# Layer 1 of a fused LSTM and quantum-circuit kernel: amplitude products on half arrays, nearest integers in SBUF, and two more buffers for low rows

## The chip, the cores and the metric

The kernel runs on one core of a Trainium2 chip. The metric is the device time of one execution in microseconds (us). The kernel before took 1453.79 us, the median of 3 runs (1453.73 to 1454.71).

## What is computed

The input x is 16 images of 128 channels and 64 x 64 pixels, f32. Two residual layers follow each other, each on a group-normalised input (32 groups of 4 channels, statistics over the image):

```python
x = x + _L0_conv_ref(_gn(x), ...)   # a diagonal LSTM: 127 dependent steps over skewed rows
x = x + _L1_conv_ref(_gn(x), ...)   # a 4-qubit circuit at every pixel
```

Layer 1 maps each pixel's 128 channels to 4 numbers, turns them into the angles of a product state of 4 qubits, applies a fixed circuit (16 complex amplitudes), takes the 4 expectations and maps them to 128 channels:

```python
xq = xf @ pre_w.T + pre_b
z = _simulate(xq, q_weights)
out = z @ post_w.T + post_b
```

The kernel writes the product state as a sum of sines of 8 signed sums of the angles. So a pixel needs 16 angles (a matmul), their sines, 32 amplitude parts (a matmul), their squares, and a last matmul to 128 channels, to which the residual is added.

## The kernel before, in words

Layer 0 takes about the first 1290 us: a load of all images with statistics, then a scan of 159 steps (`NSTEP`) whose order is written out by hand. It works in `ring`, an SBUF buffer of 40 of the 64 rows of all images. Rows 0 to 23 (`NLOW`) are finished first and stored to a DRAM buffer `low` (L605), so that later input rows can take their place. When the scan is done, rows 24 to 63 are in `ring` and rows 0 to 23 in `low`.

Beside the scan, VectorE collects the statistics of layer 1 in the tile `stats` (L122, bn_stats at L651). After the last step it reduces the last part (L628, L619, L621, L631), and a chain of small operations on VectorE, TensorE and ScalarE (L808 to L832) leaves `w_image` and `b_image`, the angle weights with the normalisation folded in.

Layer 1 goes image by image. A block of 8 rows is a tile of 128 x 512; an image has 8 of them, three low ones (`lowp`, 12 buffers) and five views of `ring`. For image b:

- `load(b)` (L848): GpSimd issues three DMAs from `low` to SBUF (L853), 256 KB each.
- `angles(b)` (L859): 8 matmuls into one PSUM tile `theta` (two buffers), each on a quarter of the array's columns, in the order of blocks 4, 6, 2, 0, then 5, 7, 3, 1. Blocks 0 to 2 are the low ones. The 128 partitions of `theta` are 8 blocks of 16 angles.
- `sines(b)` (L874): ScalarE adds `b_image` (L878); VectorE takes the nearest integer by adding and subtracting a large constant, into `theta`'s own PSUM tile (L879), and subtracts it (L880); ScalarE takes the sine (L883).
- `squares(b)` (L885): two matmuls of the full array (L889), `am0` and `am1`, each with all 128 partitions of sines as contraction; ScalarE squares both (L894). The weights `w_amp[:, h, :]` are zero outside the 64 partitions of half h, because each group of 16 partitions has its own 32 output columns (L462, `mask`).
- `outputs(b, h)` (L896): four matmuls into four PSUM tiles `po0` to `po3` (one buffer each), each on a quarter of the array's rows.
- `finish(b, h)` (L910): four VectorE operations (L917) add `po`, the bias and the residual in place, in the low tile or in `ring`. The sync engine SP stores each low tile by itself (L919) and the ring rows in one DMA per half (L922). A low tile's buffer comes free when its store has landed.

In the profile each f32 matmul is two MATMUL instructions (passes). The order of the stage is written out by hand (L927 to L955): the first four images are loaded ahead; then per image load(b+4), outputs(b,0), ScalarE's and VectorE's share of sines(b+2) around finish(b,0), squares(b+1), the sine of b+2, outputs(b,1), finish(b,1), angles(b+3). Each engine runs its instructions in that order. With 12 low buffers, the three loads of image b+4 take the buffers of the three low tiles of image b, in order.

Buffers of pools that are closed are given to pools that are opened later: `lowp`, `sinp` and `sqp` lie where the scan's pools lay, and their first writer waits for the last users there. `const` stays for the whole kernel.

Of the kernel before, what the change touches and what calls it, by code (L numbers as in the profile page):

```python
# [11 lines left out]
F32 = mybir.dt.float32  # L12
AF = mybir.ActivationFunctionType
ALU = mybir.AluOpType
PSUM = bass.MemoryType.PSUM

P = 128
NB = 16
# [8 lines left out]
CHUNK = 2 * BLOCK  # L27
# [8 lines left out]
ROUND = 12582912.0  # L36
# [43 lines left out]
def kernel(  # L80
# [16 lines left out]
    nc = tc.nc  # L97
# [3 lines left out]
    const = ctx.enter_context(tc.tile_pool(name="const", bufs=1))  # L101
# [17 lines left out]
    mean2 = const.tile([P, NB], F32, name="mean2")  # L119
    rstd2 = const.tile([P, NB], F32, name="rstd2")  # L120
    NG2 = NH // 4
    stats = const.tile([P, NB, NG2, 6], F32, name="stats")  # L122
    w_theta = const.tile([P, 128], F32, name="w_theta")
    w_image = const.tile([P, NB, 48], F32, name="w_image")
    b_image = const.tile([P, NB], F32, name="b_image")
# [1 line left out]
    w_amp = const.tile([P, 2, 128], F32, name="w_amp")  # L127
# [24 lines left out]
    with ExitStack() as scan:  # L152
        wpool = scan.enter_context(tc.tile_pool(name="wpool", bufs=1))
# [2 lines left out]
        w1T = wpool.tile([P, 512], F32, name="w1T")  # L156
        wsT = wpool.tile([P, 512], F32, name="wsT")
        bias = wpool.tile([P, 4], F32, name="bias")

        hinv = wpool.tile([P, NH], F32, name="hinv")  # L160
        cinv = wpool.tile([P, NH], F32, name="cinv")
# [36 lines left out]
        with ExitStack() as prep:  # L198
# [188 lines left out]
            for g in ORDER:  # L387
                first[g] = ps_gate.tile([P, 2, NC], F32, name=f"ps0_{g}", tag="gate")
                for w, rhs in ((w1T, hst[0][:, :, 0 : LEAST // 2]), (w0T, above(hst[0], 0, LEAST // 2))):
                    nc.tensor.matmul(  # L390
                        first[g][:, :, 0 : LEAST // 2],
                        lhsT=w[:, g * 128 : (g + 1) * 128],
                        rhs=rhs,
                        start=w is w1T,
                        stop=True,
# [398 lines left out]
        with tc.manual_schedule():  # L794
# [7 lines left out]
            k, n = 2 * FIRST, 2 * NG2  # L802
# [33 lines left out]

    lowp = ctx.enter_context(tc.tile_pool(name="lowp", bufs=12))
    sinp = ctx.enter_context(tc.tile_pool(name="sinp", bufs=3))  # L840
    sqp = ctx.enter_context(tc.tile_pool(name="sqp", bufs=2))
    ps_t = ctx.enter_context(tc.tile_pool(name="ps_t", bufs=2, space=PSUM))
    ps_a = ctx.enter_context(tc.tile_pool(name="ps_a", bufs=1, space=PSUM))
# [2 lines left out]
    x1s, ths, turns, sqs = {}, {}, {}, {}  # L846
# [27 lines left out]
    def sines(b):  # L874

        th = ths[b]
        y = sinp.tile([P, CHUNK], F32, name=f"y{b}", tag="y")
        nc.scalar.activation(y, th, AF.Identity, bias=b_image[:, b : b + 1])  # L878
        nc.vector.tensor_scalar(th, y, ROUND, ROUND, ALU.add, ALU.subtract)  # L879
        nc.vector.tensor_sub(y, y, th)  # L880
        turns[b] = y
        yield
        nc.scalar.activation(y, y, AF.Sin, scale=TWO_PI)  # L883

    def squares(b):  # L885
        ams = []
        for h in range(2):
            am = ps_a.tile([P, CHUNK], F32, name=f"am{b}_{h}", tag=f"am{h}")
            nc.tensor.matmul(am, lhsT=w_amp[:, h, :], rhs=turns[b], start=True, stop=True)  # L889
            ams.append(am)  # L890

        sqs[b] = [sqp.tile([P, CHUNK], F32, name=f"sq{b}", tag="sq"), turns[b]]
        for am, s in zip(ams, sqs[b]):
            nc.scalar.activation(s, am, AF.Square)  # L894
# [32 lines left out]
    with tc.manual_schedule():  # L927
        for b in range(4):
            load(b)
        angles(0)  # L930
        for _ in sines(0):
            pass
        angles(1)
        later = sines(1)
        next(later)
        squares(0)
        next(later, None)
        for b in range(NB):
            if b + 4 < NB:
                load(b + 4)  # L940
            po = outputs(b, 0)
            later = sines(b + 2) if 0 < b < NB - 2 else iter(())
            finish(b, 0, po)
            next(later, None)
            if b + 1 < NB:
                squares(b + 1)
            next(later, None)
            po = outputs(b, 1)
            finish(b, 1, po)
            if b == 0:  # L950
                angles(2)
                for _ in sines(2):
                    pass
            if b + 3 < NB:
                angles(b + 3)  # L955
# [37 lines left out]
```

## Time and profile before

| what | value |
|---|---|
| median of 3 runs | 1453.79 us |
| the profiled execution, its own time | 1455.38 us |
| its span in the profile | 1453.4 us |
| mean granted TensorE clock | 0.985 of full speed |
| TensorE matmul busy | 1371.0 us (94%) |
| VectorE busy | 976.8 us (67%) |
| ScalarE busy | 766.1 us (53%) |
| GpSimd busy | 897.6 us (62%) |
| HBM read, written | 59.61 MB, 46.14 MB |
| layer 1's first angle matmul starts at | 1304.1 us |
| first store of layer 1 | 1314.9 us |

How to read it: busy shares are of the whole span, of which the scan is nine tenths, so they say little about layer 1. For that stage one reads the timeline, the waits and windows from 1290 us on. In a timeline row stand start, length, engine, line, operation, output <- input, shape and count, and in square brackets the idle time before it and who ended it. The lines cited, such as L889, are those of the code above. PE is TensorE, PEld its weight loads, DVE VectorE, ACT ScalarE, POOL GpSimd, SP the engine that issues the stores.

### The profile page before, as it was taken

How to read it: one execution, taken by the hardware profiler on the slowest of the kernel's cores; microseconds unless marked ns; L12 is line 12 of the kernel's file. 1: busy time of each engine (PE TensorE's matmuls, PEld its weight loads, DVE VectorE, ACT ScalarE, POOL GpSimd, SP SyncE). 2: the span in 40 equal slices, each digit the busy share in tenths (PEclk: the TensorE clock that was granted, in tenths of full speed). 3: DMA queues.
4: the chain of work that ended last, by engine and by line, in shares of the span. 5: the costliest groups of instructions: out<-in, count | busy, mean ns of one | idle time of the engine just before them, and what ended most of it. 6: DMA issues, size and time to landing. Idle time of an engine off the chain costs nothing. (4 is left out here: it accounts for less than half of the span.)

```text
span 1453.4 us, 19718 instructions
## 1 busy us (share of the span) xinstructions
PE 1371.0 (94%) x5942; PEld 966.9 (67%) x5942; DVE 976.8 (67%) x2450; ACT 766.1 (53%) x1855; POOL 897.6 (62%) x1717
## 2 busy tenths in 40 slices
PE   6778999999999999999999999999999999858987
PEld 5648887766777667676677767776677787852222
DVE  6884566566665666877767775555555688768776
ACT  5545666555555555555555555555555565533221
POOL 4215787766777667788788766676666676531110
PEclk9999999999999999999999999999999999989997
DMA  9970000000000000144433000000000000027997
GB/s 327 362 263 1 1 1 1 1 1 1 1 0 1 1 0 1 59 136 136 134 117 116 1 0 1 2 0 1 1 1 0 1 1 1 1 88 259 332 326 269
DMA packets 86008, 107.00 MB, mean 74 GB/s; under 512 B 3936, under 2 KB 70528, under 8 KB 85904
## 3 DMA queue, kind: packets, MB, share of 16 engines
q1 hardware_dynamic: 80624, 92.29, 18.8%
q0 software_dynamic: 4048, 12.67, 2.7%
q8 instruction: 47, 0.77, 0.2%
q10 hardware_dynamic: 1232, 0.80, 0.2%
q14 instruction: 57, 0.47, 0.1%
HBM read 59.61 MB, written 46.14 MB: 73 GB/s over the span
## 5 line engine op out<-in xcount | busy, mean ns | idle before, releaser
L565 PE MATMUL ps<-xn,wxT 128*128 128x512 f32 (+18 forms) x1280 | 481.3, 519 | 1.5 <-POOL xn L556 0.9
L709 DVE TENSOR_TENSOR ps<-ps,both 128x256 f32<-128x256 f32 (+9 forms) x544 | 219.5, 408 | 318.6 <-PE ps L694 312.3
L713 ACT ACTIVATE ps<-ps,bias 128x512 f32<-128x512 f32 (+23 forms) x480 | 268.4, 581 | 254.1 <-DVE ps L709 217.5
L565 PEld LDWEIGHTS ps<-xn,wxT 128*128 128x128 f32 x1280 | 232.4, 192 | 174.9 <-issue 155.4
L739 ACT COPY both<-ps 128x256 f32<-128x256 f32 (+9 forms) x544 | 191.5, 355 | 179.9 <-PE ps L694 160.1
L694 PE MATMUL ps<-diff,w1T 128*128 128x256 f32 (+14 forms) x1088 | 284.3, 364 | 0.0
L694 PE MATMUL ps<-diff,w0T 128*128 128x256 f32 (+14 forms) x1088 | 284.1, 363 | 0.0
L599 POOL TENSOR_TENSOR ring<-ring,hst 128x256 f32<-128x256 f32 (+8 forms) x488 | 247.8, 539 | 24.4 <-DVE hst L776 24.4
L694 PEld LDWEIGHTS ps<-hst,wsT 128*128 128x128 f32 x1088 | 195.9, 190 | 86.7 <-DVE hst L776 38.1
L694 PE MATMUL ps<-hst,wsT 128*128 128x256 f32 (+14 forms) x1088 | 241.6, 365 | 6.6 <-DVE hst L776 5.0
L694 PEld LDWEIGHTS ps<-diff,w1T 128*128 128x128 f32 x1088 | 200.8, 191 | 21.0
L694 PEld LDWEIGHTS ps<-diff,w0T 128*128 128x128 f32 x1088 | 200.6, 191 | 21.0
L556 POOL TENSOR_TENSOR xn<-xn,rstd 128x512 f32<-128x512 f32 (+10 forms) x160 | 170.7, 1067 | 14.8 <-DVE rstd L149 2.3
L551 POOL TENSOR_TENSOR xn<-ring 128x256 f32<-128x256 f32 (+8 forms) x213 | 147.0, 700 | 0.0
L776 DVE TENSOR_TENSOR hst<-g,ps 128x256 f32<-128x256 f32 (+13 forms) x320 | 107.8, 368 | 46.6 <-ACT g L767 44.1
L546 POOL TENSOR_TENSOR xn<-ring,mean 128x16 f32<-128x16 f32 (+8 forms) x247 | 130.6, 538 | 11.4 <-DVE mean L139 10.4
L767 ACT ACTIVATE g<-cst 128x256 f32<-128x256 f32 (+20 forms) x320 | 102.9, 368 | 64.5 <-DVE cst L766 63.9
L590 POOL TENSOR_TENSOR diff<-hst 128x240 f32<-128x240 f32 (+9 forms) x136 | 102.9, 756 | 41.5 <-DVE hst L776 37.7
L766 DVE TENSOR_TENSOR cst<-cst,ps 128x256 f32<-128x256 f32 (+20 forms) x320 | 104.6, 368 | 5.5
L788 POOL COPY edge<-hst 128x16 f32<-128x16 f32 x64 | 25.1, 392 | 134.3 <-DVE hst L776 134.3
L763 DVE TENSOR_TENSOR ps<-ps,g 128x512 f32<-128x512 f32 (+20 forms) x160 | 95.1, 594 | 18.1 <-ACT g L713 17.1
L713 ACT ACTIVATE g<-ps,bias 128x512 f32<-128x512 f32 (+20 forms) x160 | 97.3, 608 | 11.5 <-PE ps L694 3.5
(309 smaller groups left out, 1218.3 us busy)
## 6 DMA issues: line engine op xcount, KB each, us to landing
out_dram<-ring SPq DMA_DIRECT2D x16, 1024.0 KB, 5.7
ring<-in_x_dram SPq DMA_DIRECT2D x15, 1024.0 KB, 10.1
rest<-in_x_dram SPq DMA_DIRECT2D x48, 256.0 KB, 7.8
low<-ring SPq DMA_DIRECT2D x6, 2048.0 KB, 7.6
ring<-in_x_dram SPq DMA_DIRECT2D x6, 2048.0 KB, 8.2
low<-low POOLq DMA_DIRECT2D x48, 256.0 KB, 5.2
out_dram<-low SPq DMA_DIRECT2D x48, 256.0 KB, 4.9
ring<-in_x_dram SPq DMA_DIRECT2D x20, 256.0 KB, 10.1
```

The lines of the kernel that those rows point to most:

```text
L546: nc.gpsimd.tensor_sub(by_pairs(xn, 0, j, n), x0, over(mean1, n))
L551: nc.gpsimd.tensor_sub(by_pairs(xn, 1, j, n), lower, of)
L556: nc.gpsimd.tensor_mul(v, v, r)
L565: nc.tensor.matmul(ps[g][:, :, a:b], lhsT=wxT[:, g * 128 : (g + 1) * 128], rhs=xns[t % 2][:, :, a:b], start=t > 0, stop=True, skip_group_c ...
L590: nc.gpsimd.tensor_sub(diff[:, 0, a1:b], now[:, 1, a1 - NB : b - NB], now[:, 0, a1:b])
L599: nc.gpsimd.tensor_add(x1, x1, by_pairs(new, q, j, n))
L694: nc.tensor.matmul(out, lhsT=w[:, g * 128 : (g + 1) * 128], rhs=rhs, start=False, stop=True, skip_group_check=True,)
L709: nc.vector.tensor_add(v, v, both[g][:, a:b])
L713: nc.scalar.activation(to[:, :, a:w], ps[g][:, :, a:w], FUNC[g], bias=bias[:, g : g + 1])
L739: nc.scalar.copy(both[g][:, a:b], ps[g][:, 0, a:b])
L766: nc.vector.tensor_add(c[:, q], c[:, q], ig[:, q])
L776: nc.vector.tensor_mul(new[:, q, a:v], th[:, q, a:v], act[GO][:, q, a:v])
```

## The change

Four edits, in layer 1's buffers and two of its steps:

- The tile `stats` moves from the pool `const` to `wpool`, which is closed with the scan.
- `lowp` has 14 buffers in place of 12. The three loads of image b+4 so take the buffers of low tiles 1 and 2 of image b-1 and of tile 0 of image b.
- The nearest integers go to a new SBUF tile `near` (a pool of one buffer) in place of `theta`'s PSUM tile.
- Each of the two amplitude matmuls contracts only the 64 partitions on which its weights are not zero, on rows 0 to 63 or rows 64 to 127 of the array.

The order of the stage and the number of instructions stay as they were.

```diff
-    stats = const.tile([P, NB, NG2, 6], F32, name="stats")
...
         bias = wpool.tile([P, 4], F32, name="bias")
+        stats = wpool.tile([P, NB, NG2, 6], F32, name="stats")
...
-    lowp = ctx.enter_context(tc.tile_pool(name="lowp", bufs=12))
+    lowp = ctx.enter_context(tc.tile_pool(name="lowp", bufs=14))
     sinp = ctx.enter_context(tc.tile_pool(name="sinp", bufs=3))
+    nearp = ctx.enter_context(tc.tile_pool(name="nearp", bufs=1))
...
-        nc.vector.tensor_scalar(th, y, ROUND, ROUND, ALU.add, ALU.subtract)
-        nc.vector.tensor_sub(y, y, th)
+        near = nearp.tile([P, CHUNK], F32, name=f"near{b}", tag="near")
+        nc.vector.tensor_scalar(near, y, ROUND, ROUND, ALU.add, ALU.subtract)
+        nc.vector.tensor_sub(y, y, near)
...
-            nc.tensor.matmul(am, lhsT=w_amp[:, h, :], rhs=turns[b], start=True, stop=True)
+            k = 64 * h
+            nc.tensor.matmul(
+                am,
+                lhsT=w_amp[k : k + 64, h, :],
+                rhs=turns[b][k : k + 64, :],
+                start=True,
+                stop=True,
+                tile_position=(k, 0),
+            )
```

## The prediction

> **What bounds the kernel now.** I read the slices of the page first: TensorE fills the scan (1290 us) and the change leaves that alone. It touches layer 1, the last 150 us, and the few microseconds before. Then I read the list of waits from 1304 us on (who <- for whom: us in total, times, longest):
>
> ```profile
> POOL low L853 <- DMA out_dram<-low: 42.4, 4, 19.1
> DVE low L917 <- PE po L900: 24.4, 14, 5.0
> PE theta L864 <- DMA low<-low: 10.6, 8, 2.6
> ```
>
> VectorE is late because TensorE is, and TensorE because the low rows of a coming image have not landed; GpSimd, which issues those loads, waits for a store. The timeline of image 4 shows the ring (start, length, engine, operation; the last row is image 6):
>
> ```profile
> 1347.03 2.07 DVE L917 SCALAR_TENSOR_TENSOR low<-po,b_out,low 128x512 f32<-128x512 f32 x3 [3.87 <-PE po L900]
> 1353.48 1.78 POOL L853 DMA_DIRECT2D low<-low  x3 [7.24 <-DVE ring L917]
> 1361.08 0.62 PE L864 MATMUL theta<-low,w_image 128*32 128x512 f32 x2 [0.90 <-DMA low<-low]
> 1362.92 1.14 PE L900 MATMUL po<-sq,w_out 32*128 32x512 f32 x8
> 1364.08 2.07 DVE L917 SCALAR_TENSOR_TENSOR low<-po,b_out,low 128x512 f32<-128x512 f32 x3 [2.10 <-PE po L900]
> ```
>
> finish(4,0) starts at 1347.03; its first store lands and frees a low buffer at 1353.48 (6.45 later; GpSimd's label names VectorE, but the wait also holds the store's semaphore, and finish had long written the tile); three issues take 1.78; the third tile lands 5.8 after that, at 1361.08; angles(8) and outputs(6,0), behind it in TensorE's order, let finish(6,0) start 3.0 later. That is 17.05 us for two images, 8.5 each. VectorE alone would need 6.95 (finish 2 to finish 3: 1329.51 to 1336.46). From finish(3,0) at 1336.46 to finish(13,0) at 1425.74, ten images take 89.3 us. DMA is not far behind (window; TensorE, weight loads, VectorE, ScalarE, GpSimd busy; clock, DMA share, GB/s):
>
> ```profile
> 1350.00:1356.00 6.00, 5.62 (x29) 1.44 (x28) 4.38 (x8) 1.32 (x2) 1.61 (x3) 1.00 0.72 235
> 1356.00:1362.00 6.00, 5.10 (x25) 1.52 (x25) 5.95 (x10) 1.82 (x3) 0.00 (x0) 1.00 1.06 393
> ```
>
> It reaches 393 GB/s with loads and stores mixed and starves between. An image moves 2.10 MB out and 0.79 MB in: at 393 that is 7.3 us.
>
> The start and the tail, from the timeline:
>
> ```profile
> 1291.47 5.49 POOL L853 DMA_DIRECT2D low<-low  x10 [0.36 <-POOL ring L599]
> 1299.21 0.42 DVE L631 TENSOR_REDUCE more<-stats 128x16 f32<-128x192 f32 x1
> 1304.37 1.07 PE L864 MATMUL theta<-low,w_image 128*32 128x512 f32 x2
> 1310.35 0.63 ACT L883 ACTIVATE y<-y 128x512 f32<-128x512 f32 x1 [1.48 <-DVE y L880]
> 1311.03 1.98 PE L889 MATMUL am<-y,w_amp 128*128 128x512 f32 x4 [1.27 <-ACT y L883]
> 1434.47 3.56 PE L889 MATMUL am<-y,w_amp 128*128 128x512 f32 x4
> 1439.12 2.73 DVE L917 SCALAR_TENSOR_TENSOR ring<-po,b_out,ring 128x512 f32<-128x512 f32 x4 [3.78 <-PE po L900]
> ```
>
> The first loads go out at 1291.47, 13 us before angles(0) needs them. At the end VectorE waits 3.78 us for a chain that holds am of image 15, 3.56 us long because TensorE's clock reads 0.50 there.
>
> [...] Two 64-row tiles are not in the trace, but four 32-row ones are: the eight po passes take 1.14 us, four full-array am passes 1.98. [...] The trace has 0.69 for both, with a PSUM operand; [...] after a stall of some 2 us that ends at 1389, the clock reads 0.50 from 1390 to 1392.
>
> **The change, part by part.**
> *stats moves to the pool that dies with the scan.* The build of the new kernel shows that the first load (L853) now waits for VectorE's second L631 as well: the low buffers lie where stats lay. L631 ends at 1299.63 instead of a release at 1291.47, so all twelve first loads move by 8.3 us. low_2 of image 0 is the third issue, two issues of 0.55 later; in the trace before, the third issue started at 1292.57 and had landed by 1297.32, 4.75 us. New landing: 1299.63+0.1+1.1+4.75 = 1305.6, where TensorE takes it at 1304.37. Behind that wait stand the rest of angles(0), angles(1) and everything after. Cost 1.2 to 1.5[...]: take +1.3. [...] Images 1 to 3 load well ahead and need no time.
> *near in SBUF.* L879 0.69 to 0.43, -0.26 an image; L880 stays 0.69. [...] It counts where VectorE leads: the first image, finish 1 to 2, 2 to 3. [...] near has one buffer, but writer and reader are both on VectorE, in order: no wait. theta comes free earlier; nobody waits for that.
> So finish(3,0) stands at +1.3-3x0.26 = +0.5.
> *Fourteen low buffers.* Loads of image b+4 no longer wait for stores (b,0), (b,1), (b,2), but for (b-1,1), (b-1,2), (b,0). Only tile 2 is left in the ring, released by the same store that released tile 0. Two issues leave it: -1.2. The bytes of two tiles leave the queue ahead of it: another 0 to -1.5 (0.52 MB at 350 GB/s), and more pressure on DMA gives some back. I take -1.5 per two images, 0.75 each. Of the ten intervals two (finish 9 to 11, 6.85 and 6.94) are VectorE's and gain 0.26: 8x0.75+2x0.26 = -6.5. New mean (89.3-6.5)/10 = 8.3 us an image, 348 GB/s: below 393, so it fits. Bounds: -1 (DMA is already the limit) to -12 (7.7 us an image).
> *am on half the rows each.* In mid-stage its 1.98 us are hidden: outputs(b,1) behind it waits for VectorE to free po anyway (at 1349.75 for image 4, while am ended at 1348.93). If that cover were gone it would be worth 0.9. In the tail: 3.56 to about 2.0, -1.5, and near of image 15 -0.2: -1.7. The bounds: -0.9 if the clock is full there, 0 if the tiles don't overlap.
>
> **Sum.** +0.5-6.5-1.7 = -7.7. The profiled execution took 1455.38 (span 1453.4 and 2.0 around it): 1447.7. It stood 1.6 above the median 1453.79, so for the median: 1446.1, call it 1446.
>
> **Rivals.**
> 1. DMA is already the limit, and earlier loads only displace stores. For it: shares of 0.93 to 1.05 through most windows. Against: 235 GB/s at 1350 to 1356, 393 just after. Then -1 in place of -6.5: 1453.8+0.5-1-1.7 = 1451.6, call it 1452.
> 2. The clock, and slower. Halving am takes a second of array work from each image, some 6.1 to 5.2 us of 8.3; half-clock spells then come inside the stage. For it: the clock falls in the tail as soon as angles are gone, and at 1389 after one stall. Against: in most images it held 1.00 through stalls of up to 2.6 us, and stalls shrink. A cold image needs theta 3.7, am 2.1, po 2.1 twice: 10 us, 1.7 over the 8.3. It eats the gain from about five cold images; all ten cold are +17 on the forecast: 1463. With eight cold: 1446+13.6 = 1459.6, call it 1459.
> 3. The halves don't run beside each other, so that the edit of am does nothing: the tail keeps 1.5, 1447.5. For it: no 64-row tile in the trace. Against: po's four tiles do overlap.
>
> **How the numbers follow.** Forecast 0.63 (own range 1441 to 1450.5); rival 1 0.16; rival 2 0.11; rival 3 0.10. 0.2% is 2.9 us, about what a measurement of this kernel can tell from no change: faster means under 1450.9. The forecast, rival 3 and a small part of rival 1 give 0.75 faster; the rest of rival 1 0.14 same; rival 2 0.11 slower. The range takes in the forecast, its unknown costs and most of rival 1: 1440 to 1453.
>
> **What would show it.** First load after 1299.6; angles(0) held on low to about 1305.6; L879 0.43; am's four passes about 1.1 us; the gap from finish(b,0) to finish(b+2,0) 16 to 16.6 in place of 17 to 18; finish(13,0) near 1419.7. It is wrong if the images stay at 8.9 us with DMA shares over 1.0 (rival 1), if the clock reads under 0.9 in windows between 1330 and 1420 (rival 2), or if the start costs more than 3 us.

## The result, and the profile after

The changed kernel takes 1448.08 us (median of 5 runs, 1447.33 to 1449.15); the kernel before took 1454.71 beside it (5 runs, 1453.73 to 1455.90; the three runs named further up are among them). The ratio is 0.9952, with an interval of 0.9939 to 0.9965: some 6.6 us faster, where 1446 had been predicted against 1453.79, which is 7.8. The profiled execution took 1447.33 us, its span is 1445.3; the one profiled before took 1455.38. So the two profiled executions lie 8.05 us apart, 1.4 more than the medians, and the parts read off them below add up to more than the change is worth in the median. (The scan has 160 steps, not the 159 told above; nothing rests on it.)

The list of waits of the changed kernel from 1304 us on, the three rows that answer to those shown of before:

```profile
POOL low L854 <- DMA out_dram<-low: 30.7, 9, 7.4
DVE low L928 <- PE po L911: 21.1, 14, 5.1
PE theta L865 <- DMA low<-low: 8.2, 4, 2.5
```

In total all three waits are shorter, and all three are still there: the ring from store to load to angles is eased, not gone. The start and the tail in the timeline of the changed kernel:

```profile
1298.28 0.42 DVE L631 TENSOR_REDUCE more<-stats 128x16 f32<-128x192 f32 x1
1299.42 6.03 POOL L854 DMA_DIRECT2D low<-low  x11 [9.24 <-DVE moments L808]
1304.77 1.07 PE L865 MATMUL theta<-low,w_image 128*32 128x512 f32 x2
1310.26 0.63 ACT L885 ACTIVATE y<-y 128x512 f32<-128x512 f32 x1 [1.22 <-DVE y L882]
1310.94 1.13 PE L893 MATMUL am<-y,w_amp 64*128 64x512 f32 x4 [1.06 <-ACT y L885]
1427.00 2.08 PE L893 MATMUL am<-y,w_amp 64*128 64x512 f32 x4
1429.01 1.94 PE L911 MATMUL po<-y,w_out 32*128 32x512 f32 x8
1430.97 2.73 DVE L928 SCALAR_TENSOR_TENSOR ring<-po,b_out,ring 128x512 f32<-128x512 f32 x4 [3.11 <-PE po L911]
```

The first load goes out 8.9 us later, counted from the end of the scan (9.84 in place of 0.96), after the reductions of the statistics. am's four passes take 1.13 us where the full array took 1.98, and 2.08 in the tail, at half clock, where it took 3.56. The scan, which the change leaves alone, happened to end 0.93 us earlier in this execution than in the one of before; so I count layer 1 from the last operation of the scan on VectorE (start of `hst`, 1290.51 before, 1289.58 after):

| us from the end of the scan | before | after | difference | predicted |
|---|---|---|---|---|
| angles(0) take low rows | 13.86 | 15.19 | +1.33 | +1.3 |
| finish(3,0) starts | 45.95 | 46.59 | +0.64 | +0.5 |
| finish(3,0) to finish(13,0) | 89.28 | 82.35 | -6.93 | -6.5 |
| finish(13,0) to the end of VectorE's work | 21.65 | 20.79 | -0.86 | -1.7 |
| end of the span | 162.89 | 155.72 | -7.17 | -7.7 |

The last stores take 6.0 us after VectorE's last operation in both. The third row runs from the start of finish(3,0), shown further down, to that of finish(13,0), here before and after:

```profile
1425.74 2.07 DVE L917 SCALAR_TENSOR_TENSOR low<-po,b_out,low 128x512 f32<-128x512 f32 x3 [1.76 <-PE po L900]
```

```profile
1418.52 2.07 DVE L928 SCALAR_TENSOR_TENSOR low<-po,b_out,low 128x512 f32<-128x512 f32 x3 [0.42 <-PE po L911]
```

Each figure of this table is from one execution a kernel. Other profiles with fourteen buffers, below, give 81.89 to 84.81 us in the third row.

### The profile page after: what moved, and what is told of

The parts are those of the page before. It is cut to its first block, busy times and chain, and to the rows that moved or that the text cites. A ratio compares the mean times of both kernels' runs of the same rounds, so it can differ in the third digit from the quotient of the medians.

```text
span 1445.3 us, 19732 instructions
## 1 busy us (share of the span) xinstructions
PE 1364.7 (94%) x5942; PEld 964.2 (67%) x5942; DVE 972.1 (67%) x2450; ACT 764.1 (53%) x1855; POOL 897.7 (62%) x1717
```

## The experiments

Each ratio is to the kernel before on the same chip, with its interval. "Images 3 to 13" and "tail" are the third and fourth row of the table, from the profile. The medians of the kernel before differ by chip and hour from 1454.7 to 1458.0 us, so only ratios are compared between chips.

**e1_twelve**: the changed kernel with 12 low buffers.

```diff
-    lowp = ctx.enter_context(tc.tile_pool(name="lowp", bufs=14))
+    lowp = ctx.enter_context(tc.tile_pool(name="lowp", bufs=12))
```

> The changed kernel with 12 low buffers again; near, am on half rows and the moved statistics stay. Ring theory (the fourteen buffers bring the gain): the images from finish(3,0) to finish(13,0) go back to about 8.9 us each, the start still costs about 0.7, the tail gains 0.9: 0 to 1 above the kernel before, 1454 to 1456 us. Rival (the cheaper VectorE and TensorE work brings the gain, the buffers little): it stays near the changed kernel, 1448 to 1450.

Measured: 1.0005 (0.9993 to 1.0016), as the ring theory expected. Images 3 to 13 take 91.58, even more than before. The other three edits without the buffers gain nothing.

**e2_only14**: the kernel before with 14 low buffers, and with `stats` in the pool of the scan, as in the changed kernel.

```diff
-    stats = const.tile([P, NB, NG2, 6], F32, name="stats")
...
+        stats = wpool.tile([P, NB, NG2, 6], F32, name="stats")
...
-    lowp = ctx.enter_context(tc.tile_pool(name="lowp", bufs=12))
+    lowp = ctx.enter_context(tc.tile_pool(name="lowp", bufs=14))
```

> The kernel before with the statistics moved and 14 low buffers alone: am on the full array, nearest integers in PSUM. Ring theory: nearly the whole gain, about -6.9 between images 3 and 13, +1.1 at the start, tail as before: 1448.5 to 1450. Rival (am and near bring it): within 1 us of the kernel before or slower by the start.

Measured: 0.9967 (0.9957 to 0.9976), images 3 to 13 84.81, tail 22.61. The buffers alone carry 0.33% of the changed kernel's 0.48%. Images 3 to 13 gained 4.5 in this profile, where 6.9 had been expected. The intervals from finish 1 to 2 and from 2 to 3 are 6.85 and 6.94, as before.

**e3_only_am**: the kernel before with am on half the rows each, nothing else.

```diff
-            nc.tensor.matmul(am, lhsT=w_amp[:, h, :], rhs=turns[b], start=True, stop=True)
+            k = 64 * h
+            nc.tensor.matmul(
+                am, lhsT=w_amp[k : k + 64, h, :], rhs=turns[b][k : k + 64, :],
+                start=True, stop=True, tile_position=(k, 0),
+            )
```

> The kernel before with am on half rows alone. If am is hidden in mid-stage and counts only in the tail: am of image 15 falls from 3.56 to about 2.1 us, but the array then stays at half clock through the following po, so that the tail gains 0.5 to 1: about 1454. Clock rival (less array work lets the clock fall in mid-stage): windows under 0.9 between 1330 and 1420 us and a time of 1456 or more. Rival that am sits on the ring: -0.9 for each of ten images, 1445.

Measured: 1.001 (1.000 to 1.002); images 3 to 13 89.52, as before. The time and the windows are those that the text above gives for the clock rival, not the 1454 of the first theory. Where TensorE waits longest, and the windows around it (window; TensorE, weight loads, VectorE, ScalarE, GpSimd busy; clock, DMA share, GB/s):

```profile
1344.88 1.07 PE L864 MATMUL theta<-low,w_image 128*32 128x512 f32 x2 [3.01 <-DMA low<-low]
```

```profile
1338.00:1344.00 6.00, 3.88 (x14) 1.17 (x12) 5.64 (x9) 1.71 (x3) 0.60 (x2) 0.94 1.02 341
1344.00:1350.00 6.00, 5.12 (x20) 1.08 (x20) 0.00 (x0) 0.69 (x1) 1.61 (x3) 0.50 1.06 368
...
1368.00:1374.00 6.00, 4.68 (x20) 0.98 (x24) 2.77 (x5) 0.87 (x2) 1.60 (x3) 0.72 1.07 393
```

TensorE waits for low rows across the first two windows, the clock falls to 0.50, and in the second VectorE does nothing for all 6 us. In the profile of before no window between 1320 and 1428 is under 0.82; here and in e1_twelve windows of 0.50 and of 0.72 to 0.73 lie in the stage. One such stall makes an interval of 13.41 us from one finish to the next (13.65 in e1_twelve; before, the longest is 11.69).

The mean granted clock of all executions, profiled or not, says the same. On this chip it is 0.984 over 50 executions of the kernel before, 0.980 over 22 of e3 and 0.981 over 14 of e1, but 0.985 over 21 of e2, which keeps the full am; the standard error of each is under 0.001. So with twelve buffers halving am lowers the clock. These means are of the whole span; for where it falls there are only the profiles: between finish(3,0) and finish(13,0) the clock is at half for 3.4 us before, for 10.2 here and for 17.0 in e1.

**e4_low15**: 15 low buffers, the nearest integers back in PSUM; `near`'s place in SBUF goes to the fifteenth.

```diff
-    lowp = ctx.enter_context(tc.tile_pool(name="lowp", bufs=14))
+    lowp = ctx.enter_context(tc.tile_pool(name="lowp", bufs=15))
...
-    nearp = ctx.enter_context(tc.tile_pool(name="nearp", bufs=1))
...
-        near = nearp.tile([P, CHUNK], F32, name=f"near{b}", tag="near")
-        nc.vector.tensor_scalar(near, y, ROUND, ROUND, ALU.add, ALU.subtract)
-        nc.vector.tensor_sub(y, y, near)
+        nc.vector.tensor_scalar(th, y, ROUND, ROUND, ALU.add, ALU.subtract)
+        nc.vector.tensor_sub(y, y, th)
```

> The changed kernel with 15 low buffers, for whose space the nearest integers go back to PSUM. The three loads of image b+4 then wait only for stores of image b-1, a whole image earlier. If the ring of store, load and angles still limits the changed kernel: the stalls ahead of low rows go, an image falls from 8.2 to 7.4 to 7.7 us, and the time to 1441 to 1444. If DMA bandwidth is now the limit (its share reads 1.02 to 1.07 in most windows): the mean image stays 8.1 to 8.3 us and the time 1447 to 1449.

Measured: 0.9907 (0.9890 to 0.9925), images 3 to 13 74.54. Its waits and its windows:

```profile
DVE low L926 <- PE po L909: 9.6, 14, 1.7
...
PE theta L864 <- DMA low<-low: 0.8, 2, 0.5
```

```profile
1350.00:1356.00 6.00, 6.00 (x36) 1.90 (x32) 5.80 (x10) 2.07 (x4) 1.61 (x3) 1.00 1.04 385
1356.00:1362.00 6.00, 6.00 (x28) 2.04 (x24) 5.80 (x10) 2.18 (x4) 1.07 (x2) 1.00 1.05 390
1362.00:1368.00 6.00, 6.00 (x31) 1.92 (x30) 4.84 (x9) 1.99 (x4) 0.54 (x1) 1.00 1.06 386
```

The wait of TensorE's matmuls for low rows fell from 8.2 us to 0.8, that of its weight loads, which come first, from 12.8 to 5.2. The DMA share stays over 1.0 in every window from 1338 to 1416, and 7.45 us an image with 2.88 MB is 387 GB/s: the limit that the prediction read off one window of before (393 GB/s, 7.3 us). So I take DMA to set the pace here, and not at fourteen buffers. That is argued: TensorE is busy for all of these windows too, and what speaks against it as the limit is e11 below, where 0.85 us more of its work in each image lengthens ten images by 1.4 us. A sixteenth buffer was not tried.

**e5_start**: the changed kernel with `stats` in a pool of its own that the low buffers don't overlie (opened first within the scan, with the sine pool opened ahead of `lowp`).

```diff
+        statp = scan.enter_context(tc.tile_pool(name="statp", bufs=1))
+        stats = statp.tile([P, NB, NG2, 6], F32, name="stats")
...
-        stats = wpool.tile([P, NB, NG2, 6], F32, name="stats")
...
-    lowp = ctx.enter_context(tc.tile_pool(name="lowp", bufs=14))
     sinp = ctx.enter_context(tc.tile_pool(name="sinp", bufs=3))
+    lowp = ctx.enter_context(tc.tile_pool(name="lowp", bufs=14))
```

> The changed kernel, but the statistics lie in a pool of their own, under the buffers of the sines, so that the first loads no longer wait for VectorE's last reduction. If that wait is what the start lost: first loads within 1 us of the scan's end, angles(0) takes low rows 0.3 us after the ring rows, finish(0,0) about 1.1 us earlier against the scan's end (23.3 in place of 24.3), and the whole 0.5 to 1.5 us faster than the changed kernel, 0.9945 of the kernel before. If the ring or DMA swallows the start: finish(13,0) and the time stay as in the changed kernel.

Measured: 0.9948 (0.9932 to 0.9964); the changed kernel beside it (e8) 0.9951. In its timeline the first load is back:

```profile
1291.32 5.50 POOL L855 DMA_DIRECT2D low<-low  x10 [0.36 <-POOL ring L600]
...
1304.21 1.07 PE L866 MATMUL theta<-low,w_image 128*32 128x512 f32 x2
```

From the end of the scan (1290.36 here), angles(0) take low rows at 13.85 and finish(3,0) starts at 45.29: 1.34 and 1.30 less than after the change. So the wait costs 1.3 us at the place, as told. The medians differ by 1.0, within the intervals.

**e6_tail**: the changed kernel with two more matmuls on the full array in the tail, whose result nobody reads, to keep the clock up for am of image 15.

```diff
+    def busy(n):
+        ps = ps_t.tile([P, CHUNK], F32, name="busy", tag="theta")
+        v = w_image.rearrange("p b a -> p (b a)")[:, 0:CHUNK]
+        for _ in range(n):
+            nc.tensor.matmul(ps, lhsT=w_out, rhs=v, start=True, stop=True)
...
+            elif b == NB - 3:
+                busy(2)
```

> The changed kernel with two full-array matmuls more, whose result nobody reads, after outputs(13,1), where the angles of the images before stood. If half clock is what keeps the tail long: the clock stays at 1.00 to the last am, am of image 15 takes 1.1 in place of 2.08 us, the po passes behind it 1.1 in place of 1.94, and from finish(13,0) to the last VectorE operation it is about 19.4 in place of 20.8 us. Rival (the tail is VectorE's, the clock only looks bad, and two more matmuls are in the way): 20.8 or more.

Measured: 0.9948 (0.9934 to 0.9962), 0.7 us under e8 on the same chip, which the intervals don't tell apart. The timeline of its tail:

```profile
1423.77 1.98 PE L942 MATMUL busy<-w_image,w_out 128*128 128x512 f32 x4
...
1427.47 1.13 PE L893 MATMUL am<-y,w_amp 64*128 64x512 f32 x4
...
1428.53 2.22 PE L911 MATMUL po<-y,w_out 32*128 32x512 f32 x8
```

am is at its 1.13 us. The po passes behind it take 2.22, not the 1.1 expected, but VectorE no longer waits for them: its operations follow each other without a gap there. VectorE ends 18.02 after finish(13,0), 2.8 sooner than after the change, but the last stores then need 7.24 us in place of 6.0: 1.2 of it went to the stores.

**e7_best**: 15 buffers without `near`, the statistics as in e5, the tail as in e6.

> 15 low buffers with the nearest integers in PSUM, the statistics' pool of the start experiment and the two extra matmuls in the tail, together. If the three add up: about 1.1 and 1.4 below the kernel with 15 buffers, 0.989 of the kernel before. If DMA, near its limit in the kernel with 15 buffers, takes the start's gain back: 0.990 to 0.991.

Measured: 0.9876 (0.9859 to 0.9892), 1437.44 us: it beats both kernels. Images 3 to 13 take 74.04.

**e8_changed_again**: the changed kernel, to share a chip with e5 to e7.

> The changed kernel as it is, beside the three above on the same chip: 0.995 of the kernel before, images 3 to 13 in 82 to 83 us, tail 20.8 us.

Measured: 0.9951 (0.9937 to 0.9965), as the first time.

**e9_no_near** and **e10_full_am**: the changed kernel without `near` (the last two hunks of e4), and the changed kernel with am on the full array (e3's edit undone).

> The changed kernel with the nearest integers back in theta's PSUM tile; 14 buffers and am on half rows stay. As predicted, near is worth 0.26 us where VectorE leads: finish(0,0) 0.3 to 0.5 later, the short intervals 6.94 in place of 6.84 us, 1 to 2 us slower than the changed kernel. What the runs so far suggest instead: the short intervals are a ring of TensorE and VectorE through the single po buffers, so that they stay at 6.85 without near, and only the first image loses; at most 0.7 us slower.

> The changed kernel with am on the full array again; 14 buffers and near stay. If am counts in the tail alone: am of image 15 takes about 3.5 us at half clock, the tail is 21.5 to 22.5 in place of 20.8 us, images 3 to 13 take 82 to 83.5 us, short intervals 6.9; 1 to 2 us slower than the changed kernel. If its time is on the ring too: images 3 to 13 take 85 us or more and it is 3 us slower or more.

Measured: 0.9947 (0.9931 to 0.9962) and 0.9940 (0.9920 to 0.9959). Neither edit is missed: taking either out costs nothing that shows, where 1 to 2 us had been expected for am and, by the prediction, for `near`. Images 3 to 13 are 84.57 and 82.92 in their profiles, against 82.35 and 83.01 in the two profiles of the changed kernel. In e10's tail am was expected at half clock, 3.5 us long; it is no longer than the halves were in the changed kernel:

```profile
1427.43 1.98 PE L892 MATMUL am<-y,w_amp 128*128 128x512 f32 x4
...
1429.35 1.14 PE L903 MATMUL po<-y,w_out 32*128 32x512 f32 x8
...
1430.51 2.73 DVE L920 SCALAR_TENSOR_TENSOR ring<-po,b_out,ring 128x512 f32<-128x512 f32 x4 [1.55 <-PE po L903]
```

The clock is 1.00 in its windows up to 1434, so am takes 1.98 and po 1.14, where the changed kernel had 2.08 and 1.94 at half clock. Its tail is 18.88 us, 1.9 shorter. That is one profile; e2's tail, also with the full am, was at half clock (am 3.78 us).

**e11_best_full_am** and **e12_best_no_tail**: e7 with am on the full array, and e7 without the two unread matmuls.

> The version with fifteen low buffers, nearest integers back in PSUM, statistics in a pool of their own and two unread matmuls in the tail, but with both amplitude products on the full array again (four passes 1.98 us in place of 1.13). Theory: in mid-stage am is hidden whatever the buffers, and DMA sets the pace with fifteen buffers (390 GB/s, 7.4 us an image), so images 3 to 13 take 74 to 75 us as with the halves; in the tail the clock is held, so am costs 0.9 more there at most. Time within 1 us of the version with halves, ratio to the kernel before 0.987 to 0.989. Rival: with the ring gone, TensorE's 0.9 us an image shows: 80 us or more for images 3 to 13, ratio 0.992 or above.

> The same version with the halved amplitude products, but without the two unread matmuls in the tail. Theory: the last VectorE operation comes 2 to 3 us later, because TensorE falls to half clock there, but the last stores then land in 6.0 us after it in place of 7.0 to 7.2[...]: 1 to 1.5 us slower than with them, ratio 0.988 to 0.989. Rival: the stores take the whole gain, no difference (0.9876).

Measured: 0.9878 (0.9864 to 0.9891) and 0.9894 (0.9879 to 0.9909). With am on the full array images 3 to 13 take 75.47, with the halves 74.04 and (e12) 76.87: with fifteen buffers too, am is hidden. Without the unread matmuls it is 3.3 us slower than e11 on the same chip and 2.6 slower than e7 by the ratios. The profile of e12, whose execution was the slowest of its five (1443.12), puts 2.8 in VectorE's tail and the last stores together (21.40 and 6.7, against 18.28 and 7.0 in e7). So the 1 to 1.5 expected was too low, though the intervals of e7 and e12 overlap a little.

## Why the prediction was right, point by point

**"Only tile 2 is left in the ring", 0.75 an image: right in cause, near in size.** 12 buffers in the changed kernel give back the whole gain (e1), 14 in the kernel before bring 0.33% (e2), 15 bring 0.44% more than the changed kernel (e4). Ten images gained 6.93 between the two profiles, predicted 6.5; against the same profile of before the others at fourteen buffers gain 4.5 to 7.4, so a match to 0.4 us is in part luck. The mean from finish to finish is 8.24 us, 16.5 for two images, as foretold (16 to 16.6). The ring in the changed kernel, image 4 to image 6:

```profile
1345.45 2.07 DVE L928 SCALAR_TENSOR_TENSOR low<-po,b_out,low 128x512 f32<-128x512 f32 x3 [2.86 <-PE po L911]
1354.05 1.64 POOL L854 DMA_DIRECT2D low<-low  x3 [7.43 <-DMA out_dram<-low]
1359.64 1.07 PE L865 MATMUL theta<-low,w_image 128*32 128x512 f32 x2 [2.26 <-DMA low<-low]
1363.99 2.07 DVE L928 SCALAR_TENSOR_TENSOR low<-po,b_out,low 128x512 f32<-128x512 f32 x3 [5.08 <-PE po L911]
```

The load that angles(8) wait for is now the first of the three that start at 1354.05 (tile 2 of image 8; the other two are tiles 0 and 1 of image 9), so the two issues are out of the ring, as told. It lands 5.6 later, at 1359.64. But the store before it took 8.6 us to land in place of 6.45: this is the worst pair, 18.54 us. Where it goes well nothing waits and VectorE's 6.84 stands: in the changed kernel one interval of 9.3 to 11.5 is followed by one or two of 6.84 to 7.04. The gain was foretold as an even 0.75; it came as fewer stalls.

**stats, +1.3: right.** +1.33 at angles(0); e5 takes 1.3 back at the place. That +0.64 at finish(3,0) lies near the predicted +0.5 is luck: the prediction took off 0.26 three times for `near`, and the profiles show 0.60, 0 and 0.10, of which the 0.60 is not `near`'s alone (next point). `b_image` starts at 13.43 from the end of the scan in place of 13.30, and one operation shows it, L815 with 0.31 us where it had 0.17. It has 0.31 in e1 and e4 too, but 0.17 in e2 and e10, and in e6 and e8, where the first loads go out 0.87 ahead of it as in the changed kernel: what lengthened it is not shown.

**near: the price right, the place wrong.** The groups of the changed kernel (busy us, mean ns | idle before):

```profile
L882 DVE TENSOR_TENSOR y<-y,near 128x512 f32<-128x512 f32 x16 | 11.1, 692 | 0.5
...
L881 DVE TENSOR_SCALAR near<-y 128x512 f32<-128x512 f32 x16 | 6.7, 419 | 8.4 <-ACT y L879 8.4
```

0.419 us, where 0.43 had been foretold; in the kernel before L879 and L880 both took 0.686 in the mean, and nothing in its trace showed the shorter time. But the step "It counts where VectorE leads: ... finish 1 to 2, 2 to 3" failed. Here is finish(3,0), two such intervals on, first in the changed kernel and then in the kernel before (the figure in brackets is the wait for po):

```profile
1336.17 2.07 DVE L928 SCALAR_TENSOR_TENSOR low<-po,b_out,low 128x512 f32<-128x512 f32 x3 [0.42 <-PE po L911]
```

```profile
1336.46 2.07 DVE L917 SCALAR_TENSOR_TENSOR low<-po,b_out,low 128x512 f32<-128x512 f32 x3 [0.20 <-PE po L900]
```

The wait for po grew from 0.20 to 0.42. The interval from finish 1 to 2 stayed at 6.84, and that from 2 to 3 fell from 6.95 to 6.85 only. The likely reason is that VectorE didn't lead there alone: po has one buffer each, so TensorE's next outputs wait for VectorE's finish and VectorE for them (from 1304 us on in the changed kernel, the weight loads for po wait 14.5 us for VectorE's low operations and 9.9 for its ring ones, VectorE 21.1 and 3.4 for po). With the full am and no `near` such intervals are 6.84 to 6.95 (before, e11); halving am without `near` gives 6.84 to 6.85 (e4, e9), `near` with the full am 6.84 to 6.85 too (e10), and both together no less. So the two terms of -0.26 were 0 and -0.10, and not near's alone. At the first image, where VectorE waits for nobody else, finish(0,0) starts 9.14 us after angles(0) take their rows, in place of 9.74. The halved am, which the sum left out at this place, has a share in it: without `near` it is 9.35 (e9), with the full am 9.32 (e10), and a repeat of the changed kernel has 9.37 (e8). What `near` is worth in all, e9 bounds: taking it out lowered the ratio by 0.0004 ± some 0.002. The profiles leave 2 us open: with fourteen buffers images 3 to 13 take 84.81 and 84.57 in the two without `near` (e2, e9) and 81.89 to 83.48 in the five with it.

**am: the tiles overlap, the tail gave back half.** Four passes in 1.13 us in place of 1.98: 1.75 times as fast. In the trace of before only po's four tiles had shown such an overlap (eight passes in 1.14). In mid-stage it was hidden, as told (e10, e11). The term that was mis-sized is the tail's -1.7, which came to -0.86. am of image 15 did fall by 1.48 (3.56 to 2.08), as worked out. But the sum left out what stands behind it in TensorE's order: before, the clock rose during the long am (0.50 up to 1437, 1.00 from 1438), and the po passes that follow took 1.14 us; after, they came at half clock (0.50 from 1424 to 1430, 1.00 from 1431) and took 1.94 (shown above). Before:

```profile
1437.96 1.14 PE L900 MATMUL po<-y,w_out 32*128 32x512 f32 x8
```

So 0.8 went back, and VectorE's wait fell from 3.78 to 3.11 only. How much the halves are worth in the tail is not settled: with them and without the unread matmuls it takes 20.8 to 21.4 us in all eight profiles, with the full am 18.88 (e10), 21.65 (before) and 22.61 (e2), as the clock happens to fall.

**The rivals.** The first, DMA already the limit, is out: 14 buffers gained what the ring theory said, and a further buffer gained again. It may be true at 15 (387 GB/s). The third, halves that don't overlap, is out (1.13 us). The second, the clock, was half true and is what I had underrated (the halves take 0.9 us of array work from each image; the prediction writes "a second" for about a microsecond). Its sign in the tail was read too early: before, the last angles end at 1424.6, but the clock reads 1.00 up to 1430 and 0.50 from 1431. Its image of 10 us was an estimate; at half clock, in the tail of the changed kernel, am takes 2.08 and po 1.94, near the 2.1 assumed for each. With 12 buffers it costs at least what am brings (e3). In the changed kernel the clock is at half for part of one window of the stage, just where the ring rows above stall:

```profile
1356.00:1362.00 6.00, 3.74 (x15) 0.71 (x16) 2.91 (x5) 0.63 (x1) 1.07 (x2) 0.75 1.02 322
1362.00:1368.00 6.00, 6.00 (x28) 1.94 (x28) 3.98 (x7) 1.97 (x4) 0.54 (x1) 0.97 1.06 399
```

The theta passes at 1359.64 take 1.07 a pair in place of 0.62, and the interval 11.50 us. The prediction had called a clock under 0.9 in a window there a sign that it is wrong; one such window cost at most a few us of one interval and not the gain, and the kernel before has a window of 0.82 there itself, so the sign could not tell the two apart. With fourteen buffers the clock is at half for some 3.4 us between finish(3,0) and finish(13,0), where e1 has 17.0. That halving am lowers the clock is shown with twelve buffers, by e3 against the kernel before. With fourteen it is not: e10, with the full am, has a window of 0.74 in the stage too (1374 to 1380), and the mean clocks, 0.983 to 0.984 with the halves (changed kernel, e8, e9) and 0.985 and 0.986 with the full am (e2, e10), come from different chips.

**What stays open.** e2's 0.9967 and the changed kernel's 0.9951 lie 0.16% apart on different chips, so `near` and am together may be worth 2 us or nothing. Against e2, `near` alone (e10, 0.9940) and am alone (e9, 0.9947) look worth 0.2 to 0.3% each, about as much as the intervals leave open; against the changed kernel, taking either out costs nothing. The two don't fit together, and no run here says which is the stray.

## What to carry to other kernels

Where a load waits for a store that waits for the work before it, count the buffers first: two more were worth 0.33% alone and 0.53% within the changed kernel (e1), and a third one about 0.4% more, by which time DMA ran at 387 GB/s, while edits that made single instructions 1.6 to 1.75 times faster could each be taken out of the changed kernel without a loss that shows. Before you count a faster instruction as a gain, read what waits behind it in its engine's order and at which clock that will run; and when a tile moves into a pool that is closed early, look who inherits its place (here the first loads, 8.9 us later, of which 1.3 us reached the chain).

## What the runs showed of the hardware

- Loads and stores mixed held 385 to 390 GB/s over three windows of 6 us on one core (e4, 1350 to 1368), with a DMA share of 1.04 to 1.06; over the windows from 1338 to 1416 they read 333 to 392.
- A wait of TensorE was at times followed by half clock. After waits for low rows of 3.01 us (e3, to 1344.88), 2.26 us (the changed kernel, to 1359.64) and 2.16 us (before, to 1389.07) windows read 0.50, 0.75 and, over 1390 to 1392, 0.50. After others of 2.63 us (before, to 1344.03) and 1.40 us (the changed kernel, to 1342.45) the clock stayed at 1.00, so the length of a wait alone doesn't decide it; what does stays open.
- Two unread matmuls, 1.98 us in all, ahead of the last two images: with them am of image 15 ran at full clock in all three profiles (1.13 us in e6 and e7, 1.98 in e11, in windows that read 1.00); without them all or most of it ran at half clock in ten of eleven (the exception is e10). By the medians they were worth 0.7 us in e6 (e8 less e6, not told apart from nothing) and 2.6 with fifteen buffers (e12 against e7, by the ratios).
- Two matmuls of 64 rows each, on the two halves of the array, took 1.13 us for four passes at full clock, where two on all 128 rows took 1.98.
